# Two graph-network layers by nested fast matrix products: S4 written graph by graph, two sums of y behind VectorE's adds, first aggregations mixed with the next P1, variances of the last tiles on ScalarE

## The chip, the cores and the metric

The kernel runs on one core of one Trainium2 chip. The metric is the device time of one execution in microseconds: the median of three runs before the change is 1888.36 us (1888.13 to 1889.2). All matrix products are fp32. TensorE multiplies into the eight banks of PSUM (called `bank` in the profile), VectorE (DVE) and ScalarE (ACT) read and write the banks, GpSimd (POOL) works on SBUF only, and SyncE (SP) issues the transfers.

## The reference

64 graphs of 256 nodes with 512 features, two layers, each with a residual and a layer norm. Cut to what matters:

```python
def _L0_gnn_ref(x, adj, W):
    deg = jnp.sum(adj, axis=-1, keepdims=True)
    agg = jnp.einsum('bij,bjf->bif', adj, x) / jnp.maximum(deg, EPS)
    cat = jnp.concatenate([x, agg], axis=2)
    return jax.nn.relu(jnp.einsum('bnf,of->bno', cat, W))

def _L1_gnn_ref(X, adj, mask, Wqk, Wv):
    q, k = jnp.split(X @ Wqk, 2, axis=-1)
    v = X @ Wv
    agg = jnp.einsum('bij,bjd->bid', adj, k * mask[:, :, None])
    w = inv_scale * mask * jnp.einsum('bid,bid->bi', q, agg)
    return jax.nn.softmax(w, axis=1)[:, :, None] * v

x = _layernorm(x + _L0_gnn_ref(x, adj, L0_gnn_W), axis=-1)
x = _layernorm(x + _L1_gnn_ref(x, adj, nodemask, L1_gnn_Wqk, L1_gnn_Wv), axis=-1)
```

## The kernel before: the parts that the change and the prediction touch

The graphs go through in 32 pairs. In iteration j, layer 0 of pair j and layer 1 of pair j-1 are interleaved product by product. A product with weights is done by a scheme of seven products, P1 to P7, where four of them (P1, P2, P3, P5) are split by the same scheme again. The scheme needs sums of the left side (S1 to S4) and of the right side (T1 to T4). S1 to S3 are made on VectorE or GpSimd, S4 on GpSimd. S4 is stored over a sum that is no longer needed: over S1 for the input of layer 0 (`xT_s`), over S2 for that of layer 1 (`x1T_s`).

```python
def block(self, s, ks):          # a sum or a block of the input, for graphs ks
    return self.s[:, ks, self.slot[s]] if isinstance(s, int) else self.a[:, ks, s[0], :, s[1]]

def fourth_sums(X):
    ks = slice(0, 2)
    gp.tensor_sub(X.block(S4, ks), X.block(A12, ks), X.block(S2, ks))
    inner_sums(X, gp, 2)         # four smaller sums of S4, for P3
```

The work is ordered by lists of small steps; `run("a b c")` takes the next step of each list named. A step issues one or more products (`mm`), then the copies and adds of its result, then `tick()`, which issues waiting steps of other chains (norms, masks, weight sums) to VectorE and ScalarE as far as a model of their load allows; `flush(name)` issues the rest of a chain at once.

The products P1, P2, P5 and P3 (`inner`) have four steps each. P1 and P5 end with VectorE's adds to two banks; then P1's banks `u` are copied by ScalarE, before P6 (the products with S2, `pairs(u, X, S2, ...)`) adds onto the same banks:

```python
def last_two():
    mm(q[1][:, :HF], X.chunk(block, 1, 1), b["T4"])
    mm(q[0][:, HF:], s(3), b["B22"])
    if p in ("P1", "P5"):
        for k in range(2):
            vec.tensor_add(q[k][:, HF:], q[k][:, HF:], fifth[0])   # bank<-bank,fifth
    done(fifth[0])
    tick()

def after_p1(fifth):
    for k in range(2):
        act.copy(own[:, k, 0], u[k])                               # own<-bank
```

An aggregation (`gather`) multiplies the adjacency (`adj`, with sums `sa`) with a right side (here y, with sums `tv`) by one level of the scheme, with steps a to g:

```python
def sums_T(val, later=None):
    ...
    vec.tensor_sub(t1, b12, b11)
    rest = [lambda args=args: vec.tensor_sub(*args) for args in ((t2, b22, t1), (t3, b22, b12), (t4, b21, t2))]
    if later is None:
        for do in rest:
            do()
    else:
        later.extend(rest)       # issued by spare(), one each in a, b and d

def onto(t, ps):                 # adds a bank to own, scaled by 1/degree
    for k in range(2):
        r = own[:, k, t, :HF]
        vec.scalar_tensor_tensor(r, ps[:, k * HF:(k + 1) * HF], rdeg[:, k, t:t + 1], r, op0=OP.mult, op1=OP.add)

def u1():                        # a
    twice(u, "A11", "B11")
    ...  onto(0, u)
    spare(); tick()
def g2():                        # b
    twice(p2, "A12", "B21")
    ...  onto(0, p2)
    spare(); tick()
def g5():                        # c
    twice(p5, "S1", "T1")
    tick()
def u2():                        # d: adds onto the bank of a
    twice(u, "S2", "T2", start=False)
    act.copy(r12, of(u))
    spare(); tick()
def u3():                        # e
    twice(u, "S3", "T3", start=False)
    act.copy(r22, of(u))
    vec.tensor_add(r22, of(p5), r22)
    tick()
# f = g3 (S4·B22 onto p5), g = u4 (A22·T4 onto u)
```

The main loop, cut (i, k, m, r are P1, P5, P2, P3 of layer 0; p, q, s are P6, P7, P4; j there is P1 of layer 1):

```python
for j in range(NP):
    ...
    if j == 0:
        run("i k i k i k i k", i=i, k=k)
        ...
    elif j == 1:
        early.append(a1)
        run("k i k i k i k", i=early[0], k=k)      # one step of P1 was done at j == 0
        fourth_sums(X)
        run("m p p m p p m", m=m, p=p)
        load_x(1)
    else:
        run("i k", i=i, k=k)
        ...
        run("i l k", i=i, k=k, l=open1)
        flush("norm")
        ...
        run("i k i k", i=i, k=k)
    if j != 1:
        fourth_sums(X)
    ...
    run("r q r m", m=m, q=q, r=r)
    if j == 1:
        flush("norm", "mask")
        sumsM[0] = adj_sums(0)
        load_rows(2)
    ...
    T_late = []
    T = sums_T(ys[j], T_late if j < 2 else None)
    g = gather(sumsA.pop(j), T, zs[j], pw[1], y[1], y[0], owns[j], rdegs[j], T_late)
    if j == 0:
        ...
        run("s s a b s d c e i g f", s=s, i=early[0], **g)
    elif j == 1:                                    # (an else in the kernel)
        turn_here(Y, owns[0], 0, pw)
        run("s", s=s)
        turn_here(Y, owns[0], 1, pw)
        ...
        run("s b a s d c", s=s, **g)
        ...
    else:
        run("s s j s a b", s=s, j=jj, k=k, **g)
        run("j", j=jj)
        ...
        run("c d j k e j", s=s, j=jj, k=k, **g)
```

The end, for layer 1 of the last pair: `b3` adds P3 and its fifth product (`fifth`) to v (here `x`); `probs` is the softmax; x1 (`own`) is the residual and the output.

```python
run("r", r=r)
flush()
for k in range(2):
    last[k][0](pw[k])                    # probabilities: total x fifth
b3(held[0])                              # per k: v += y[k]; v[HF:] += fifth
for k in range(2):
    vec.tensor_copy(probs[j][:, k], pw[k][:, :NT])
for t in (1, 0):
    for k in range(2):
        o = x1[:, k, t:t + 1]
        vec.scalar_tensor_tensor(o[:, 0], vs[j][k][:, t], probs[j][:, k, t:t + 1], o[:, 0], op0=OP.mult, op1=OP.add)
        stats, scale = layer_norm(o, ..., 1, (t, k) == (0, 1))    # bn_stats, bn_aggr; Ln, Exp; shift; scaling
        run_now(stats + scale[:1])
        norms.append((k, t, scale[1:]))
        if len(norms) == 2:
            close(*norms.pop(0))         # shift, scaling, transfer of the tile
close(*norms.pop(0))
```

Of the kernel before, what the change touches and what calls it, by code (L numbers as in the profile page):

```python
# [46 lines left out]
A11, A21, A12, A22 = ((u, v) for u in range(2) for v in range(2))  # L47
S1, S2, S3, S4 = range(4)
# [46 lines left out]
def resnorm_kernel(  # L95
# [15 lines left out]
    NT, NF, NA = N // P, F // P, A // P  # L111
    H, HF = NF // 2, F // 2
# [7 lines left out]
    small = ctx.enter_context(tc.tile_pool(name="small", bufs=4))  # L120
# [55 lines left out]
    def first(out, in_):  # L176

        return tc.keep_in_program_order(nc.sync.dma_start(out, in_))
# [10 lines left out]
    def load_rows(j):  # L189
        rows[j] = pool.tile([P, 2 * NT * F], F32, name="turn")[:, :2 * NT * N].rearrange(  # L190
            "p (k t n) -> p k t n", k=2, t=NT)
        for k in range(2):
            first(rows[j][:, k], adj[2 * j + k].rearrange("(t p) j -> p t j", p=P))
# [88 lines left out]

    def fourth_sums(X):

        ks = slice(0, 2)
        gp.tensor_sub(X.block(S4, ks), X.block(A12, ks), X.block(S2, ks))
        inner_sums(X, gp, 2)

    def run_now(steps):
        for _, work in steps:  # L290
            work()
# [13 lines left out]
    def adj_sums(j):  # L305
        a, s = adjs[j], pool.tile([P, 4, 2, P], F32, name="sa", bufs=2)
        a11, a21, a12, a22 = (a[:, :, t, h * P:(h + 1) * P] for t in range(2) for h in range(2))
        gp.tensor_add(s[:, 0], a21, a22)
        gp.tensor_sub(s[:, 1], s[:, 0], a11)
        gp.tensor_sub(s[:, 2], a11, a21)  # L310
        gp.tensor_sub(s[:, 3], a12, s[:, 1])
        return {"A11": a11, "A12": a12, "A22": a22, "S1": s[:, 0], "S2": s[:, 1], "S3": s[:, 2], "S4": s[:, 3]}
# [71 lines left out]
            return go  # L384
        return [unit(e) for e in range(H)]

    def sums_T(val, later=None):

        b11, b12, b21, b22 = (val[:, :, t, h * HF:(h + 1) * HF] for t in range(NT) for h in range(2))
        tv = pool.tile([P, 4, 2, HF], F32, name="tv")  # L390
        t1, t2, t3, t4 = (tv[:, r] for r in range(4))
        vec.tensor_sub(t1, b12, b11)
        rest = [lambda args=args: vec.tensor_sub(*args) for args in ((t2, b22, t1), (t3, b22, b12), (t4, b21, t2))]
        if later is None:
            for do in rest:
                do()
        else:
            later.extend(rest)
        return {"B11": b11, "B21": b21, "B22": b22, "T1": t1, "T2": t2, "T3": t3, "T4": t4}

    def gather(a, w, dst, u, p5, p2, own=None, rdeg=None, later=()):
# [69 lines left out]
        return dict(a=[u1], b=[g2], c=[g5], d=[u2], e=[u3], f=[g3], g=[u4])  # L471


    def norm_of(src, total):

        rstd, shift, less, var = (small.tile([P, NT], F32, name=x) for x in ("rstd", "shift", "less", "var"))

        def mean():
            vec.tensor_scalar(less, total, -1.0 / F, None, op0=OP.mult)

        def square(t):
            junk = small.tile([P, F], BF16, name="junk", bufs=1)
            act.activation(junk, src[:, t], AF.Square, bias=less[:, t:t + 1], accum_out=var[:, t:t + 1])

        def factor():
            act.activation(rstd, var, AF.Ln, bias=eps, scale=1.0 / F)
            act.activation(rstd, rstd, AF.Exp, scale=-0.5)

        def shifts():
            vec.tensor_tensor(shift, less, rstd, op=OP.mult)  # L490

        def scale(t):
            act.activation(src[:, t], src[:, t], AF.Identity, bias=shift[:, t:t + 1], scale=rstd[:, t:t + 1])
        return [(vec, mean)] + [(act, lambda t=t: square(t)) for t in range(NT)] + [(act, factor), (vec, shifts)] + [
            (act, lambda t=t: scale(t)) for t in range(NT)]

    def layer_norm(src, mv, n, by_vec):

# [255 lines left out]
    for j in range(NP):  # L754
# [17 lines left out]
        if j == 0:  # L772
            run("i k i k i k i k", i=i, k=k)
            flush("degrees")
            load_rows(1)
        elif j == 1:
            early.append(a1)
            run("k i k i k i k", i=early[0], k=k)
            fourth_sums(X)
            run("m p p m p p m", m=m, p=p)  # L780
            load_x(1)
        else:
            run("i k", i=i, k=k)
            send_scores(j - 2)
            run("i l k", i=i, k=k, l=open1)
            flush("norm")
            fetch_scores(j - 2)
            places[0](range(16))
            run("i k i k", i=i, k=k)
# [15 lines left out]
        flush("w0")  # L805
        run("r q r m", m=m, q=q, r=r)
        if j == 1:
            flush("norm", "mask")
            sumsM[0] = adj_sums(0)
            load_rows(2)  # L810
        quiet[0] = j < 2
        room[vec] = -9.0 if j > 1 else 0.6
        run("r s r", r=r, s=s)
# [3 lines left out]
            inner_sums(Y, gp, 0)  # L817
            queue(1, "sums", *outer_sums(Y, vec), (vec, lambda Y=Y: inner_sums(Y, gp, 1)))
        T_late = []
        T = sums_T(ys[j], T_late if j < 2 else None)  # L820

        if j == 0:
            degrees(1)
# [11 lines left out]
        if j == 0:  # L835
            sums_next()
            held = [c for c in chains if c[1] == "w1"]
            chains[:] = [c for c in chains if c[1] != "w1"]
            early.append(inner("P1", Xs[1], W0, pw[0], u, lambda fifth: early[1](fifth)))
            run("s s a b s d c e i g f", s=s, i=early[0], **g)  # L840
            quiet[0] = False
        else:
            u2, o2, y2 = o, pf, y
            b1, b2, b3, b4, b5, b6, b7, b8 = layer1(j - 1, ys[j][:, :, 0], o2, u2, y2)
            jj = inner("P1", Y, W1, pw[0], u2)
            k = inner("P2", Y, W1, y[0], o2, b2)
            if j == 1:
                turn_here(Y, owns[0], 0, pw)
                run("s", s=s)
                turn_here(Y, owns[0], 1, pw)  # L850
                inner_sums(Y, gp, 0)
                sums_Y = (*outer_sums(Y, vec), (vec, lambda: inner_sums(Y, gp, 1)))
                run("s b a s d c", s=s, **g)
                quiet[0] = False
                flush("w1")
                run("e j g f", j=jj, **g)
                queue(1, "sums", *sums_Y)
                run("k j k j k j", j=jj, k=k)
                b1(None)
                run("k", k=k)  # L860
            else:
                run("s s j s a b", s=s, j=jj, k=k, **g)
                room[vec] = 0.6
                run("j", j=jj)
                if j < NP - 1:
                    degrees(j + 1)
                run("c d j k e j", s=s, j=jj, k=k, **g)
                quiet[0] = True
                run("k", k=k)
                quiet[0] = False  # L870
                b1(None)
                run("g f", **g)
# [78 lines left out]
    for _, turn, exps in last:  # L951
        turn()
        exps()
    run("r", r=r)
    flush()
    probs[j] = small.tile([P, 2, NT], F32, name="probs", bufs=2)
    for k in range(2):
        last[k][0](pw[k])
    b3(held[0])
    for k in range(2):  # L960
        vec.tensor_copy(probs[j][:, k], pw[k][:, :NT])
    norms = []

    def close(k, t, scale):
        for _, work in scale:
            work()
        first(out[2 * j + k, t * P:(t + 1) * P], x1[:, k, t])
    for t in (1, 0):
        for k in range(2):
            o = x1[:, k, t:t + 1]  # L970
            vec.scalar_tensor_tensor(o[:, 0], vs[j][k][:, t], probs[j][:, k, t:t + 1], o[:, 0],
                                     op0=OP.mult, op1=OP.add)
            stats, scale = layer_norm(o, small.tile([P, 1, 2], F32, name="mv"), 1, (t, k) == (0, 1))
            run_now(stats + scale[:1])
            norms.append((k, t, scale[1:]))
            if len(norms) == 2:
                close(*norms.pop(0))
    close(*norms.pop(0))


# [24 lines left out]
```

## Time and profile before

| | before |
|---|---|
| median of 3 runs | 1888.36 us |
| span of the profiled execution | 1884.5 us |
| TensorE busy | 1861.3 us (99%) |
| VectorE busy | 1541.9 us (82%) |
| ScalarE busy | 1303.6 us (69%) |
| GpSimd busy | 896.5 us (48%) |
| mean granted TensorE clock | 0.997 |
| transfers | 181.26 MB, 96 GB/s in the mean |

The profile is a page of one execution, with views that can be asked for beside it: the waits (who waited for whom, total, times, longest), the chain of waits that ended last, the timeline (instructions of each engine in order of time: start, length, engine, line, operation, output<-input, shapes, how many were merged, and in brackets the idle time before and what ended it) and the instructions of one tile. The names are those of the program without buffer numbers: `xT_s` are the sums S of the input, `xT_i` the smaller sums for the inner scheme, `tv` the sums T of an aggregation, `sa` the sums of the adjacency, `own` the residual stream of a pair, `fifth` the fifth inner product. Almost all instructions carry the line of a helper, so groups are told apart by tiles.

### The profile page before, as it was taken

What the parts mean: (1) busy time and instruction counts of PE and PEld (TensorE: products, weight loads), DVE (VectorE), ACT (ScalarE), POOL (GpSimd) and SP (SyncE); (2) the same over time, 40 slices, a digit from 0 to 9 for tenths busy, and PEclk for the clock granted to TensorE, in tenths of its full rate; (3) what the DMA queues carried; (4) which work ended last, traced back from release to release, by engine and by line L of the source; (5) the groups of instructions that cost most, each with busy time, mean ns of one, the idle gap of its engine ahead of it and who ended that gap; (6) DMA issues with size and microseconds to landing.
All of it is one profiled execution on the core that took longest, in us unless ns stands there. A gap on an engine that the chain in (4) does not pass through costs nothing.

```text
span 1884.5 us, 24896 instructions
## 1 busy us (share of the span) xinstructions
PE 1861.3 (99%) x6996; PEld 1312.9 (70%) x6996; DVE 1541.9 (82%) x3182; ACT 1303.6 (69%) x3270; POOL 896.5 (48%) x1187
## 2 busy tenths in 40 slices
PE   9999999999999999999999999999999999999997
PEld 5667767767777677677677677676776777776764
DVE  7787888788888878887888888788878888878887
ACT  3667776677776677766777776777676777667765
POOL 4455453555454554435554435454445544355532
PEclk9999999999999999999999999999999999999998
DMA  6133334333333333343433343333434233433321
GB/s 225 56 74 81 99 90 118 85 97 92 103 96 103 100 83 97 90 118 85 104 88 101 96 114 89 84 98 95 112 85 108 84 102 95 118 85 88 98 62 51
DMA packets 380713, 181.26 MB, mean 96 GB/s; under 512 B 263712, under 2 KB 345248, under 8 KB 380576
## 3 DMA queue, kind: packets, MB, share of 16 engines
q1 hardware_dynamic: 380576, 179.67, 35.5%
q8 instruction: 57, 0.93, 0.2%
q14 instruction: 80, 0.66, 0.1%
HBM read 114.10 MB, written 34.06 MB: 79 GB/s over the span
## 4 chain that ended last, share of the span: by engine, by line
PE 92%; DVE 5%; ACT 1%; POOL 1%; issue 1%; DMA 0%; DVEq 0%; ACTq 0%
PE bank L173 92%; DVE own L90 2%; DVE tv L90 1%; DVE y L90 1%; POOL xT_s L90 1%; ACT y L90 0%; ACT own L90 0%; DMA wqk<-wqk_t 0%; PE bank L625 0%; ACT bank L90 0%; DVE st L90 0%; DVE t L90 0%; DVE x L90 0%; DVE v L90 0%; ACT junk L90 0%
## 5 line engine op out<-in xcount | busy, mean ns | idle before, releaser
L90 ACT COPY bank<-bank 128x256 f32<-128x256 f32 (+1 forms) x768 | 332.6, 436 | 241.0 <-PE bank L173 231.9
L90 DVE TENSOR_TENSOR y<-bank,y 128x512 f32<-128x512 f32 x256 | 170.6, 687 | 133.2 <-ACT y L90 132.2
L90 ACT ACTIVATE junk<-own,less 128x512 bf16<-128x512 f32 x252 | 182.5, 724 | 64.8 <-DVE less L90 63.9
L90 ACT ACTIVATE own<-own,shift,rstd 128x512 f32<-128x512 f32 x255 | 200.4, 812 | 0.0
L173 PE MATMUL bank<-tv,sa 128*128 128x256 f32 x768 | 194.7, 381 | 4.0 <-DVE tv L90 1.8
L90 POOL TENSOR_TENSOR x1T_s<-x1T,x1T_s 128x512 f32<-128x512 f32 x32 | 53.2, 1663 | 280.9 <-PE bank L173 280.9
L173 PEld LDWEIGHTS bank<-tv,sa 128*128 128x128 f32 x768 | 144.8, 190 | 56.0 <-issue 22.9
L90 ACT COPY y<-bank 128x512 f32<-128x512 f32 x192 | 108.9, 584 | 94.9 <-PE bank L173 93.5
L90 POOL TENSOR_TENSOR sa<-adj 128x256 f32<-128x256 f32 x128 | 95.6, 747 | 159.3 <-DMA adj<-adj_t 150.5
L173 PE MATMUL bank<-w,x1T_s 128*128 128x512 f32 (+1 forms) x384 | 168.4, 521 | 0.0
L90 POOL TENSOR_TENSOR x1T_i<-x1T 128x256 f32<-128x256 f32 x64 | 55.6, 868 | 228.6 <-DMA x1T<-turn 213.3
L173 PE MATMUL bank<-t,xT_s 128*128 128x512 f32 (+1 forms) x384 | 160.2, 526 | 2.4 <-POOL xT_s L90 1.5
L90 POOL TENSOR_TENSOR x1T_i<-x1T_s 128x128 f32<-128x128 f32 x128 | 76.6, 598 | 177.4 <-DVE x1T_s L90 174.9
L90 DVE TENSOR_TENSOR v<-bank,v 128x512 f32<-128x512 f32 x186 | 119.2, 683 | 48.8 <-PE bank L173 48.8
L173 PE MATMUL bank<-t,x1T_s 128*128 128x512 f32 (+1 forms) x384 | 158.2, 522 | 0.3 <-ACT y L90 0.3
L173 PE MATMUL bank<-w,xT_s 128*128 128x512 f32 (+1 forms) x384 | 153.2, 521 | 0.0
L173 PE MATMUL bank<-t_i,xT_i 128*128 128x256 f32 x512 | 152.7, 380 | 0.4 <-POOL sa L90 0.2
L173 PE MATMUL bank<-t_i,x1T_i 128*128 128x256 f32 x512 | 152.3, 379 | 0.1
L173 PEld LDWEIGHTS bank<-t_i,x1T_i 128*128 128x128 f32 x512 | 97.2, 190 | 67.0 <-issue 49.7
L90 ACT COPY own<-bank 128x512 f32<-128x512 f32 x128 | 71.8, 587 | 93.5 <-PE bank L173 49.4
L173 PEld LDWEIGHTS bank<-t_i,xT_i 128*128 128x128 f32 x512 | 94.9, 190 | 58.1 <-issue 46.3
L173 PE MATMUL bank<-t,x1T 128*128 128x512 f32 x256 | 130.5, 593 | 0.0
(156 smaller groups left out, 4610.1 us busy)
## 6 DMA issues: line engine op xcount, KB each, us to landing
x<-x SPq DMA_DIRECT2D x64, 512.0 KB, 5.7
xT<-x_t SPq DMA_DIRECT2D x62, 512.0 KB, 5.5
out<-own SPq DMA_DIRECT2D x62, 512.0 KB, 3.2
x1T<-turn SPq DMA_DIRECT2D x480, 64.0 KB, 2.3
adj<-adj_t SPq DMA_DIRECT2D x64, 256.0 KB, 3.8
turn<-adj SPq DMA_DIRECT2D x64, 256.0 KB, 3.0
row<-d SPq DMA_DIRECT2D x31, 256.0 KB, 4.7
wqk<-wqk_t SPq DMA_DIRECT2D x4, 512.0 KB, 5.3
```

What stands on the lines that cost most here:

```text
L90: return self.tc.keep_in_program_order(getattr(self.engine, name)(out, *args, **kwargs))
L173: tc.keep_in_program_order(nc.tensor.matmul(ps, a, b, start=start, stop=True, skip_group_check=True))
```

## The change

Six edits. S4 is subtracted for one graph after the other, so that the first half can start before the reads of the second graph's old sum are done. For the pairs from 2 on, T3 and T4 of y are issued behind VectorE's adds of the aggregation to `own` instead of ahead of them. In the first iteration S1·T1 (c) is issued ahead of S2·T2 (d), and one more step of the next pair's P1 stands between the aggregation's steps; in the second the aggregation starts with a instead of b, P2's first step comes ahead of P5's last, and the flush of the masks, the sums of the masked adjacency and a load come after the first turning of the norm's output. At the end P3's fifth product is added by an identity product on TensorE, P3's adds are split, and the variances of two of the last four tiles are taken by ScalarE's square with its accumulator instead of VectorE's statistics.

```diff
     def fourth_sums(X):
-        ks = slice(0, 2)
-        gp.tensor_sub(X.block(S4, ks), X.block(A12, ks), X.block(S2, ks))
+        for k in (slice(0, 1), slice(1, 2)):
+            gp.tensor_sub(X.block(S4, k), X.block(A12, k), X.block(S2, k))
         inner_sums(X, gp, 2)
...
-    def sums_T(val, later=None):
+    def sums_T(val, later=None, n=3):
...
-        if later is None:
-            for do in rest:
-                do()
-        else:
-            later.extend(rest)
+        for do in rest[:n]:
+            do()
+        if n < len(rest):
+            later.extend(rest[n:])
...
-            run("k i k i k i k", i=early[0], k=k)
+            run("k i k i k m k", i=early[0], k=k, m=m)
             fourth_sums(X)
-            run("m p p m p p m", m=m, p=p)
+            run("p p m p p m", m=m, p=p)
...
         if j == 1:
-            flush("norm", "mask")
-            sumsM[0] = adj_sums(0)
-            load_rows(2)
+            flush("norm")
...
-        T = sums_T(ys[j], T_late if j < 2 else None)
+        T = sums_T(ys[j], T_late, 0 if j < 2 else 1)
...
-            run("s s a b s d c e i g f", s=s, i=early[0], **g)
+            run("s s a b s c d i e i g f", s=s, i=early[0], **g)
...
                 turn_here(Y, owns[0], 0, pw)
+                flush("mask")
+                sumsM[0] = adj_sums(0)
+                load_rows(2)
...
-                run("s b a s d c", s=s, **g)
+                run("s a b s d c", s=s, **g)
...
     run("r", r=r)
+    for k in range(2):
+        mm(y[k][:, HF:], ident, held[0])
     flush()
...
-    b3(held[0])
+    def add_p3(k):
+        vec.tensor_add(vs[j][k][:, 0], y[k], vs[j][k][:, 0])
+    def stt(k, t, **more):
+        vec.scalar_tensor_tensor(x1[:, k, t], vs[j][k][:, t], probs[j][:, k, t:t + 1], x1[:, k, t],
+                                 op0=OP.mult, op1=OP.add, **more)
...
+    add_p3(0)
     for k in range(2):
         vec.tensor_copy(probs[j][:, k], pw[k][:, :NT])
     norms = []
-    for t in (1, 0):
-        for k in range(2):
-            ...                      # the loop shown above
+    for k in range(2):
+        total = small.tile([P, 1], F32, name="total2", bufs=2)
+        stt(k, 1, accum_out=total)
+        steps = norm_of(x1[:, k, 1:2], total, 1)     # mean; square, Ln and Exp on ScalarE; shift; scaling
+        run_now(steps[:3])
+        norms.append((k, 1, steps[3:]))
+    add_p3(1)
+    for k in range(2):
+        stt(k, 0)
+        stats, scale = layer_norm(x1[:, k, 0:1], small.tile([P, 1, 2], F32, name="mv"), 1, k == 1)
+        run_now(stats)
+        close(*norms.pop(0))
+        run_now(scale[:1])
+        norms.append((k, 0, scale[1:]))
+    for norm in norms:
+        close(*norm)
```

More of the change, by code (lines that the diff above doesn't have):

```diff
@@ L471, in gather, with norm_of @@
         return dict(a=[u1], b=[g2], c=[g5], d=[u2], e=[u3], f=[g3], g=[u4])
-    def norm_of(src, total):
-        rstd, shift, less, var = (small.tile([P, NT], F32, name=x) for x in ("rstd", "shift", "less", "var"))
+    def norm_of(src, total, n=NT):
+        rstd, shift, less, var = (small.tile([P, n], F32, name=x) for x in ("rstd", "shift", "less", "var"))
         def mean():
@@ L493, in scale @@
             act.activation(src[:, t], src[:, t], AF.Identity, bias=shift[:, t:t + 1], scale=rstd[:, t:t + 1])
-        return [(vec, mean)] + [(act, lambda t=t: square(t)) for t in range(NT)] + [(act, factor), (vec, shifts)] + [
-            (act, lambda t=t: scale(t)) for t in range(NT)]
+        return [(vec, mean)] + [(act, lambda t=t: square(t)) for t in range(n)] + [(act, factor), (vec, shifts)] + [
+            (act, lambda t=t: scale(t)) for t in range(n)]
     def layer_norm(src, mv, n, by_vec):
@@ L958, in resnorm_kernel, with close @@
         last[k][0](pw[k])
-    b3(held[0])
+    def add_p3(k):
[3 more added lines that the diff above has]
+                                 op0=OP.mult, op1=OP.add, **more)
+    def close(k, t, scale):
+        run_now(scale)
+        first(out[2 * j + k, t * P:(t + 1) * P], x1[:, k, t])
+    add_p3(0)
     for k in range(2):
@@ L962, in resnorm_kernel @@
     norms = []
[L964 to L967, printed above, removed]
-    for t in (1, 0):
-        for k in range(2):
[L970 to L978, printed above, removed]
+    for k in range(2):
[14 more added lines that the diff above has]
+        close(*norm)
 def kernel(x, adj, nodemask, L0_gnn_W, L1_gnn_Wqk, L1_gnn_Wv):
```

## The prediction

> **What bounds the kernel now.** I read the page first. TensorE is busy in 99% of the span, the others in 82% or less, so only TensorE's idle time, and what lies after its last matmul, can be won.
>
> ```profile
> PE 1861.3 (99%) x6996; PEld 1312.9 (70%) x6996; DVE 1541.9 (82%) x3182; ACT 1303.6 (69%) x3270; POOL 896.5 (48%) x1187
> ```
>
> Then the waits of TensorE (total, times, longest):
>
> ```profile
> PE bank L173 <- DVE tv L90: 1.8, 1, 1.8
> ...
> PE bank L173 <- POOL xT_s L90: 1.5, 9, 0.2
> ...
> PE bank L173 <- DVE own L90: 1.1, 1, 1.1
> ```
>
> They are small because the ends of matmuls are modelled. Starts tell more: in undisturbed stretches each record of 256 columns starts 0.215 us after the one before, each of 512 columns 0.43 us, and a product in the program is two records. I took from each pair of successive starts in the trace what goes beyond that. It comes to 34 us: 10 in the first 100 us, 21.5 in the steady part, 3 after 1836 us. The steady part has three places in a pair of graphs:
> - before the first product of S2 (t,xT_s): 19 of 30 pairs, about 0.3 us and a late second record each, 7.2 us in all;
> - in the first steps of P5 (t,xT_i), 0.2 us in each pair, 5.9 us, behind ScalarE's copy of a bank;
> - inside the first aggregation, between T1·S1 and T2·S2 (tv,sa), in ten pairs, 3.45 us in all.
>
> The first place is what "POOL xT_s" in the waits points at. Here is a pair with the gap, from the timeline (start, length, engine):
>
> ```profile
> 1726.79 0.92 DVE L90 TENSOR_TENSOR v<-v,fifth 128x256 f32<-128x256 f32 x1
> ...
> 1728.63 1.27 POOL L90 TENSOR_TENSOR xT_s<-xT,xT_s 128x512 f32<-128x512 f32 x1 [1.20 <-PE bank L173]
> ...
> 1728.86 1.39 DVE L90 TENSOR_TENSOR bank<-bank,fifth 128x256 f32<-128x256 f32 x4
> ...
> 1729.28 1.07 ACT L90 COPY own<-bank 128x512 f32<-128x512 f32 x2 [1.57 <-DVE bank L90]
> ...
> 1730.01 1.96 PE L173 MATMUL bank<-t,xT_s 128*128 128x512 f32 x4 [0.17 <-POOL xT_s L90]
> ```
>
> and one without:
>
> ```profile
> 1671.57 1.27 POOL L90 TENSOR_TENSOR xT_s<-xT,xT_s 128x512 f32<-128x512 f32 x1 [1.85 <-PE bank L173]
> ...
> 1672.62 1.88 PE L173 MATMUL bank<-t,xT_s 128*128 128x512 f32 x4
> ```
>
> In the second the product starts at 1672.62, while GpSimd's S4 runs until 1672.84. So the product doesn't wait for S4. In every pair with the gap the first copy of own ends 0.14 us before the product, to the hundredth; S4 ends anywhere from 0.21 before to 0.06 after it. The wait is for ScalarE's copy of u, which is behind VectorE's adds to the banks, which are behind `v<-v,fifth`, 0.92 us here and 0.42 to 0.46 in the pair without the gap.
>
> The third place:
>
> ```profile
> 1516.60 1.10 DVE L90 TENSOR_TENSOR tv<-y 128x512 f32<-128x512 f32 x1
> ...
> 1518.35 0.68 DVE L90 TENSOR_TENSOR tv<-y 128x512 f32<-128x512 f32 x1
> ...
> 1518.95 0.68 DVE L90 TENSOR_TENSOR tv<-y,tv 128x512 f32<-128x512 f32 x1
> 1519.32 2.28 PE L173 MATMUL bank<-tv,sa 128*128 128x256 f32 x8
> ...
> 1519.55 1.65 DVE L90 SCALAR_TENSOR_TENSOR own<-bank,rdeg,own 128x256 f32<-128x256 f32 x4
> ```
>
> The eight matmuls take 2.28 us instead of 1.88 (seven starts and a last one of 0.38): T2·S2 adds onto the bank that the adds to own must have read. T3 (1518.35) and T4 (1518.95) stand ahead of those adds, and no product needs them yet.
>
> **What the Trainium skill says.** "Perfetto Trace Analysis", section "Tensor Engine Instruction (MATMUL, LD_WEIGHTS)": the end of a matmul in a profile is a model, not an observation. The trace agrees: records of 0.38 us start 0.215 apart, hence my use of starts. "SBUF — State Buffer", section "Who interferes with whom": a VectorE instruction with two SBUF inputs contends with a GpSimd instruction that reads SBUF, and whichever issues first holds the pair for its whole length; with one SBUF input it doesn't. The trace agrees: `v<-v,fifth` takes 0.424 us at least and 1.014 at most, `own<-z,rdeg,own` 0.47 to 1.50, while `v<-bank,v`, with one input in a bank, stays at 0.68 to 0.69. "Perfetto Trace Analysis", section "Optimizing Scalar/DVE Operations": breaking up an instruction may let work be completed sooner if an engine isn't saturated but causes bubbles. GpSimd's 128x512 takes 1.27 us and its 128x256 0.73, so two halves cost 0.19 us more. "PSUM — Partial Sum Buffer", section "The four PSUM rules": a matmul without the first flag adds to what the bank holds; that is how the identity product can add the fifth. Before's trace has no such add to compare.
>
> **The change part by part.**
>
> *S4 by graph.* 64 subtractions of 1.27 us or more become 128 of about 0.73: 64 x 0.19 = 12 us more on an engine that is idle half the time. For xT the first half waits for one product of P5 less, so S4 ends about 0.55 us earlier; for x1T the first half moves some 3.5 us ahead, beside VectorE's T sums, and the second blocks `own<-z` half as long. No matmul waits for either. I give it 0, for the gap at S2 has another cause.
>
> *Later sums.* For pairs from 2 on, T3 and T4 go behind the adds of own. VectorE reaches those adds two times 0.61 us = 1.2 earlier, or when the first aggregation's product is done; the gap is 0.3 us plus a 0.11 restart. So all ten vanish: 3.4 us. T3 is then ready about 0.7 us after the adds, two products or more before its use.
>
> *First aggregations.* At pair 0:
>
> ```profile
> 46.83 2.94 PE L173 MATMUL bank<-tv,sa 128*128 128x256 f32 x12 [1.76 <-DVE tv L90]
> ```
>
> The wait is for T2, which is slow (1.65 us, beside GpSimd). S1·T1 needs T1 alone and now goes into the wait: 0.86 of 1.93 us. But u4 then has only one product of P1 ahead of it (0.43 us) while ScalarE reads the bank, where it had 0.86: 0.4 back. So 0.45, and 0.15 at the restart after it. With two steps of P1 done ahead, and P2's first step ahead of P5's last, the 0.27 waits at 53.78 and 58.88 and some restarts go: 0.6. At pair 1:
>
> ```profile
> 80.12 0.86 DVE L90 SCALAR_TENSOR_TENSOR own<-bank,rdeg,own 128x256 f32<-128x256 f32 x2
> ...
> 81.03 2.94 PE L173 MATMUL bank<-tv,sa 128*128 128x256 f32 x12 [1.15 <-DVE own L90]
> ```
>
> T2·S2 waits for u's adds behind those of the other bank, because b runs ahead of a. With a ahead of b they start at 78.2, T2 ends at 80.2 instead, and the wait shrinks by 0.8. Moving the masks' flush should help little: in the timeline the last two masks (69.85) are ahead of the own scalings (70.66), so ticks had issued them already. I give 0.3 of the 0.83 at 71.44. Sum of the head: 0.45 + 0.15 + 0.6 + 0.8 + 0.3 = 2.3 us.
>
> *The end.*
>
> ```profile
> 1870.29 1.05 PE L648 MATMUL bank<-total,fifth 1*128 1x1 f32 x8
> ...
> 1871.31 0.43 DVE L90 TENSOR_TENSOR x<-x,fifth 128x256 f32<-128x256 f32 x1
> ...
> 1872.37 0.42 DVE L90 TENSOR_TENSOR x<-x,fifth 128x256 f32<-128x256 f32 x1
> ...
> 1872.90 0.75 DVE L90 SCALAR_TENSOR_TENSOR own<-x,probs,own 128x512 f32<-128x512 f32 x1
> ...
> 1880.27 0.55 DVE L90 TENSOR_SCALAR own<-own,rstd,shift 128x512 f32<-128x512 f32 x1
> ```
>
> Two identity products (0.86 us, from 1869.95) push the probabilities' matmuls from 1870.29 to 1870.8, done at 1871.85. VectorE has one add (0.66) by then, copies, and starts the first weighted add at 1872.1: 0.8 earlier. From there before took 7.9 us to the end of the last scaling: four tiles of 1.62 (add 0.79, statistics 0.73, aggregate 0.10), then factor, shift, scaling. After: adds 0.9 each with their mean for two tiles, the second P3 add 0.62, then two tiles of 1.62, ending at +5.8 instead of +6.6. But ScalarE now runs scale(1,1), 0.73, ahead of the last factor, 0.5, and the last scaling (0.55) follows: +7.9 again. So the end gains 0.8, all at its start, and the last transfer (3.7 us) stays.
>
> Sum: 3.4 + 2.3 + 0.8 = 6.5; 1888.4 - 6.5 = 1881.9.
>
> **The rivals.** (1) S4 does hold the S2 products, as the chain of waits has it ("POOL xT_s" 0.9% of the span). Then halving it removes 7.2 us more: 1875. For it: the ends of S4 lie near the starts in all 19 pairs. Against: the pairs without gap start before S4 ends. (2) More GpSimd instructions, moved earlier, hit VectorE's two-input adds at worse moments, and the S2 gap appears in all 30 pairs: 11 x 0.37 = 4 us back, 1886. For it: the gap comes from just such a collision. Against: the earlier half lands beside transposes, whose lengths stay at 0.66 to 0.71. (3) T3 and T4 late make a new wait at u3 or hold VectorE for the x1T sums: each pair would lose 0.2, 6 us, and the gain is gone: 1888. Against: a slack of over 2 us at u3.
>
> **Range and chances.** The T gaps are sure to 0.5, the head to 1.2, the end to 0.6, S4 to 2 either way. 1878.5 to 1885.0 holds 8 in 10. 2% is 38 us, more than all of TensorE's 34 us of gaps: within 2% 0.98, each side 0.01.
>
> **What would show it.** The trace after: T2·S2 directly behind T1·S1 in all pairs from 2 on; the wait "DVE tv" near 1.0 and "DVE own" near 0.4; the S2 gaps still in about 20 pairs, 0.14 us behind the copy of own; the first weighted add of the last pair about 2.3 us after the last product of P3, not 2.9. Wrong if the S2 gaps are gone (rival 1), are in all pairs (rival 2), or T3 shows up as a releaser (rival 3).

## The result, and the profile after

The changed kernel takes 1903.35 us (median of four runs, 1901.88 to 1907.0) against 1888.24 us for the kernel before on the same chip: a ratio of 1.0083, with a 95% interval of 1.0065 to 1.01. It is 15 us slower, where 6.5 us less had been predicted, and lies outside the range of 1878.5 to 1885.0.

The profiled execution of the changed kernel is the slowest of its four (1907.0 us, span 1905.2; 1884.5 before), so the waits read from it add up to more than the medians differ by. Its line of busy times:

```profile
PE 1874.2 (98%) x7000; PEld 1308.8 (69%) x7000; DVE 1560.8 (82%) x3180; ACT 1307.5 (69%) x3274; POOL 909.8 (48%) x1251
```

No engine has become a bound: VectorE's 19 us more and GpSimd's 13 us more are a per cent of the span or less, and TensorE is still busy in 98% of it. What has changed shows in the chain that ended last, here by line:

```profile
PE bank L173 70%; DVE own L90 8%; DVE tv L90 3%; DVE y L90 3%; ACT junk L90 2%; DVE less L90 2%; ACT own L90 1%; DVE v L90 1%; DVE z L90 1%; DVE agg L90 1%; ACT agg L90 1%; POOL xT_i L90 1%; ACT bank L90 0%; POOL xT_s L90 0%; DVE turn L90 0%
```

TensorE's products carried 92% of this chain before, and carry 70% now. Names stand in it that the page of before doesn't list among its fifteen: `less` (minus the mean, in layer 0's norm), `agg` (the copies in layer 1's aggregation), `xT_i` (GpSimd's inner sums). The waits of TensorE (total us, number of times, longest) say where the chain comes back to it:

```profile
PE bank L173 <- ACT agg L90: 6.8, 25, 0.4
PE bank L173 <- ACT own L90: 5.6, 10, 0.8
PE bank L173 <- ACT bank L90: 2.8, 5, 1.2
```

"ACT agg" is new: 25 waits of some 0.3 us. "ACT own" is the old gap in front of the S2 products. To see all of it I again took from each pair of successive matmul starts what goes beyond the spacing of undisturbed ones (0.215 us for 256 columns, 0.43 for 512):

| us beyond back-to-back starts | before | after |
|---|---|---|
| first 100 us | 9.9 | 9.9 |
| steady part | 21.6 | 43.2 |
| - u4 of layer 1's aggregation (tv,adj), and the restarts behind it | 0 | 19.5, 25 pairs |
| - first S2 product (t,xT_s), and its restart | 7.3, 21 pairs | 12.9, 28 pairs |
| - T2·S2 in layer 0's aggregation (tv,sa) | 3.5, 10 pairs | 0 |
| - first steps of P5 | 5.9 | 5.9 |
| from 48.5 us ahead of the end to the last matmul | 2.9 | 2.7 |
| last matmul's start to the end of the span | 13.4 | 11.8 |

So the T gap went as predicted, and two things came: a wait at u4 that wasn't there at all, and more of the S2 gap. (At u4 the wait itself is 0.44 us on average; the next few matmuls start late too, which makes it 0.78 per pair. What the places listed leave of the steady part, some 4.9 us before and after alike, is mostly rounding: undisturbed starts lie nearer to 0.2155 and 0.431 us apart.)

The wait at u4 in one pair, in the timeline after (start, length, engine; lines of VectorE, GpSimd, ScalarE and TensorE in order of start):

```profile
1661.88 0.84 POOL L90 TENSOR_TENSOR x1T_s<-x1T,x1T_s 128x256 f32<-128x256 f32 x1 [4.99 <-PE bank L173]
...
1671.81 1.10 DVE L90 SCALAR_TENSOR_TENSOR own<-own,x 128x512 f32<-128x512 f32 x1
...
1672.32 1.71 POOL L90 TENSOR_TENSOR xT_s<-xT 128x512 f32<-128x512 f32 x1
...
1672.95 1.11 DVE L90 TENSOR_SCALAR less<-sum 128x2 f32<-128x2 f32 x1
...
1674.09 0.72 ACT L90 ACTIVATE junk<-own,less 128x512 bf16<-128x512 f32 x1 [1.94 <-DVE less L90]
...
1675.66 0.56 ACT L90 COPY agg<-bank 128x512 f32<-128x512 f32 x1
...
1676.27 1.13 PE L173 MATMUL bank<-tv,adj 128*128 128x256 f32 x4 [0.26 <-ACT agg L90]
```

and the same place in the timeline before:

```profile
1647.68 1.67 POOL L90 TENSOR_TENSOR x1T_s<-x1T,x1T_s 128x512 f32<-128x512 f32 x1 [9.10 <-PE bank L173]
...
1654.55 0.57 DVE L90 TENSOR_SCALAR less<-sum 128x2 f32<-128x2 f32 x1
...
1655.15 0.72 ACT L90 ACTIVATE junk<-own,less 128x512 bf16<-128x512 f32 x1 [0.59 <-DVE less L90]
...
1655.74 1.26 POOL L90 TENSOR_TENSOR xT_s<-xT 128x512 f32<-128x512 f32 x1
...
1656.72 0.57 ACT L90 COPY agg<-bank 128x512 f32<-128x512 f32 x1
...
1658.20 1.03 PE L173 MATMUL bank<-tv,adj 128*128 128x256 f32 x4
```

Read the two from the bottom. u4 adds onto a bank that ScalarE must have copied to `agg`. Two squares of layer 0's norm (`junk<-own,less`) stand ahead of that copy in ScalarE's queue, and in all 30 pairs it starts as the second of them ends (0.09 us ahead of the recorded end). The squares need `less`, two numbers per partition that VectorE makes. Before, `less` starts 1.19 us ahead of `xT_s<-xT`, GpSimd's first large sum for the next pair, and takes 0.57. After, `xT_s<-xT` starts 0.63 us ahead of `less`, which takes 1.11 and ends 0.03 behind it. The order of two neighbours has been swapped; everything behind them in the chain is 1.3 us later against TensorE, and the slack of 0.9 us that u4 had is gone.

### The profile page after: what moved, and what is told of

Its sections match the earlier page's. It is cut to its first block, busy times and chain, and to the rows that moved or that the text cites. A ratio compares the mean times of both kernels' runs of the same rounds, so it can differ in the third digit from the quotient of the medians.

```text
span 1905.2 us, 25004 instructions
## 1 busy us (share of the span) xinstructions
PE 1874.2 (98%) x7000; PEld 1308.8 (69%) x7000; DVE 1560.8 (82%) x3180; ACT 1307.5 (69%) x3274; POOL 909.8 (48%) x1251
## 4 chain that ended last, share of the span: by engine, by line
PE 70%; DVE 19%; ACT 5%; issue 4%; POOL 1%; DMA 0%; DVEq 0%; SPq 0%; POOLq 0%; ACTq 0%
PE bank L173 70%; DVE own L90 8%; DVE tv L90 3%; DVE y L90 3%; ACT junk L90 2%; DVE less L90 2%; ACT own L90 1%; DVE v L90 1%; DVE z L90 1%; DVE agg L90 1%; ACT agg L90 1%; POOL xT_i L90 1%; ACT bank L90 0%; POOL xT_s L90 0%; DVE turn L90 0%
## 5 line engine op out<-in xcount | busy, mean ns | idle before, releaser
L90 POOL TENSOR_TENSOR x1T_i<-x1T_s 128x128 f32<-128x128 f32 x128 | 98.3, 768 | 189.6 <-DVE x1T_s L90 187.1
L90 POOL TENSOR_TENSOR x1T_s<-x1T,x1T_s 128x256 f32<-128x256 f32 x64 | 51.7, 808 | 239.7 <-PE bank L173 239.7
```

The costliest lines, as they stand in the source:

```text
L90: return self.tc.keep_in_program_order(getattr(self.engine, name)(out, *args, **kwargs))
```

## The experiments

The theory formed from this: **GpSimd gets ahead**. The first half of S4 for layer 1 (`x1T_s`) waits for an earlier product only, and starts 3.5 us sooner. Then S4 as a whole ends sooner, and so does each of GpSimd's later sums, the next pair's among them; they now fall onto the end of VectorE's norm, and hold `less`. The rivals: **the early half itself**, which hits another VectorE instruction where it now lies; **GpSimd's additional work** (two instructions of 128x256 cost more than one of 128x512, whenever they come); **the other parts** of the change; and, for the S2 gap, the halves of layer 0's S4 or GpSimd's sums of the adjacency (`sa`).

All medians, with the ratio to the kernel before on the same chip:

| what runs | us | before | ratio, 95% |
|---|---|---|---|
| before + S4 in halves | 1911.68 | 1887.5 | 1.0126 [1.0111, 1.0141] |
| after, S4 whole | 1883.63 | 1887.5 | 0.9983 [0.9974, 0.9992] |
| after, halves in layer 0 alone | 1885.58 | 1887.5 | 0.9989 [0.998, 0.9998] |
| after, halves in layer 1 alone | 1901.19 | 1887.5 | 1.0073 [1.0058, 1.0088] |
| after, layer 1's second half first | 1882.03 | 1887.05 | 0.9973 [0.9961, 0.9986] |
| after, next pair's S1 in halves too | 1891.94 | 1887.05 | 1.0025 [1.0016, 1.0035] |
| after, one product more between u3 and u4 | 1916.05 | 1887.05 | 1.0149 [1.0134, 1.0165] |
| S4 whole, load of adj issued earlier | 1883.6 | 1887.05 | 0.9981 [0.9974, 0.9989] |
| S4 whole, sums of adj later | 1877.24 | 1887.33 | 0.9946 [0.9934, 0.9959] |
| after, sums of adj later | 1892.93 | 1887.33 | 1.0028 [1.0017, 1.0039] |
| before + late T3 and T4 | 1883.83 | 1887.33 | 0.9983 [0.9975, 0.9991] |
| S4 whole, sums of adj later, old head | 1875.19 | 1887.33 | 0.9937 [0.9922, 0.9952] |

### Which part costs the time

S4 in halves put into the kernel before, alone:

```diff
-        ks = slice(0, 2)
-        gp.tensor_sub(X.block(S4, ks), X.block(A12, ks), X.block(S2, ks))
+        for k in (slice(0, 1), slice(1, 2)):
+            gp.tensor_sub(X.block(S4, k), X.block(A12, k), X.block(S2, k))
```

> The kernel before with S4 written graph by graph in both layers and nothing else. Theory A (the halves of S4 cost all of it, by collisions of GpSimd with VectorE's two-input and small instructions): the new wait for ScalarE's copy of agg (tv,adj, 19.5 us with its restarts in the trace after) and the longer waits ahead of the S2 products (5.6 us more) appear here too, the T2 waits of 3.4 us stay: 1888 + 25 = 1910 to 1914. Theory B (the late T3 and T4 shift VectorE and so cause the new wait): no wait for the copy of agg, 1888 to 1890.

and taken out of the kernel after (the same lines the other way round):

> The changed kernel with S4 written for both graphs in one instruction again. Theory A: the wait for the copy of agg is gone in all pairs, the S2 waits are back at about 7 us with their restarts, the T2 waits stay gone, the end keeps its 0.8 us: 1883 to 1885. Theory B: 1900 or more.

Measured: 24.2 us slower than before, and 3.9 us faster than before. The halves are the whole loss, and the other parts together gain. In the first, the wait at u4 is in 29 pairs and takes 22.0 us with its restarts; in the second one wait is left, at one pair. In the waits of TensorE, after with S4 whole:

```profile
PE bank L173 <- ACT agg L90: 0.8, 1, 0.8
```

Then layer by layer, from after:

```diff
-        for k in (slice(0, 1), slice(1, 2)):
+        halves = (slice(0, 1), slice(1, 2)) if X.name == "xT" else (slice(0, 2),)
+        for k in halves:
```

> The changed kernel with S4 in halves for layer 0's sums (xT_s) alone. Theory A: only the S2 waits grow, 1884 + 5.6 = 1889 to 1890, no wait for the copy of agg. If the two places feed each other by the time at which GpSimd's sums run, there are some waits for agg too and the time is 1892 or more.

and with `"x1T"` in the place of `"xT"`:

> The changed kernel with S4 in halves for layer 1's sums (x1T_s) alone. Theory A: the wait for the copy of agg in about 25 pairs, S2 waits as in the kernel before: 1884 + 19.5 = 1903 to 1904. If layer 0's halves cause the agg wait, 1884 to 1886.

Measured from after with S4 whole: layer 0's halves cost 1.9 us (one of its twelve runs took 4008 us; without it the median is 1885.42), layer 1's 17.6. Together that is 19.5, against 19.0 for both (15.1 slower than before, where S4 whole is 3.9 faster). The two intervals overlap, so the 1.9 alone isn't sure; the traces bear it out. Layer 1's halves bring the wait at u4 in 21 pairs, 16.2 us with restarts, and 2.1 us more at S2; layer 0's bring none of the first, and 2.7 us more at S2, about half of what was expected of them.

### Early, or more?

The same two instructions, the same total, but nothing early: the half that waits for the later product goes first, and GpSimd, which works in order, holds the other behind it (S4 then starts at 5.41 us and not at 1.96, in the table below).

```diff
-        for k in (slice(0, 1), slice(1, 2)):
+        halves = (slice(0, 1), slice(1, 2)) if X.name == "xT" else (slice(1, 2), slice(0, 1))
+        for k in halves:
```

> The changed kernel, but layer 1's S4 with the second graph's half first, so that the early half can't start before the last read of S2. Theory A1 (the early start brings all of GpSimd's later sums forward, and they hit VectorE's end of the norm chain): the sums of the next x start as late as before the change, the wait for the copy of agg is gone or in a few pairs only, 1885 to 1889. Theory A2 (more and shorter GpSimd instructions as such collide more often): the wait stays, 1900 to 1905.

Measured: 1882.03, as fast as with S4 whole, and no wait at u4 is left. It isn't the work: 64 instructions of 128x256 in layer 1 cost nothing where they end late. Its timeline at the same pair:

```profile
1645.91 2.00 POOL L90 TENSOR_TENSOR x1T_s<-x1T,x1T_s 128x256 f32<-128x256 f32 x2 [8.44 <-PE bank L173]
...
1652.24 0.57 DVE L90 TENSOR_SCALAR less<-sum 128x2 f32<-128x2 f32 x1
...
1654.12 1.26 POOL L90 TENSOR_TENSOR xT_s<-xT 128x512 f32<-128x512 f32 x1
...
1656.44 1.03 PE L173 MATMUL bank<-tv,adj 128*128 128x256 f32 x4
```

`less` is ahead of `xT_s<-xT` again, by 1.88 us. The positions in all pairs, as medians in us from the first 128x512 product of layer 1's S2 (t,x1T_s); before, all 30 pairs lie within 0.16 us of them:

| | before | after | S4 whole | second half first | S1 in halves too |
|---|---|---|---|---|---|
| S4 starts | 5.41 | 1.96 | 5.41 | 5.41 | 1.96 |
| S4 done | 7.08 | 6.13 | 7.07 | 7.40 | 6.13 |
| first sum for the next pair starts | 9.51 | 8.98 | 9.51 | 10.24 | 8.89 |
| next pair's S1 (xT_s<-xT) starts | 13.46 | 12.39 | 13.46 | 13.61 | 12.39 |
| VectorE's second `less` starts | 12.28 | 13.02 | 12.27 | 11.74 | 13.01 |
| its length | 0.57 | 1.11 | 0.57 | 0.57 | 0.57 |
| ScalarE's copy to agg starts | 14.44 | 15.72 | 14.44 | 13.91 | 15.18 |
| u4 starts | 15.93 | 16.34 | 15.93 | 15.93 | 15.93 |

Down the column "after": S4 is done 0.95 us earlier, the next pair's S1 starts 1.07 earlier, `less` ends 1.28 later (0.74 at its start, 0.54 in its length), the copy to agg is 1.28 later, u4 0.41. The 0.74 come from two VectorE instructions just ahead of `less`, which run beside GpSimd's sums for the next pair: `own<-own,x` takes 1.10 instead of 0.83 and `own<-z,rdeg,own` 1.02 instead of 0.47 (medians), while VectorE had been 0.08 ahead. The early half itself isn't the cause: it does hold one of VectorE's T sums (`tv<-own,tv`, 1.22 instead of 0.68), but VectorE's first `less` starts at 8.18, where before it was 8.27.

The pairs of the kernel after show it among themselves. In 25 of its 30 the next pair's S1 starts at 12.38 to 12.54, `less` takes 1.11 and u4 starts late, at 16.33 to 16.5. In four S1 starts at 13.24 or later, `less` is ahead of it and takes 0.56 or 0.57, and u4 starts at 15.93. In the last there is no next pair: 0.17, and 15.93 again. No pair is an exception.

### The link between S1 and `less`

If `less` is held for as long as S1 runs, a shorter S1 must release it sooner:

```diff
-            run_now(rest[:1])
+            for ks in (slice(0, 1), slice(1, 2)):
+                run_now(outer_sums(Xs[j + 1], gp, ks)[:1])
```

> The changed kernel with the next pair's S1 (128x512 on GpSimd) also written graph by graph. If it is this one long instruction that holds VectorE's small mean (less, 1.1 us instead of 0.2 to 0.6) and through it ScalarE's squares and the copy of agg: the mean waits 0.7 us at most, the copy comes about 0.5 us earlier, the wait for it goes in most pairs, 1886 to 1893. If the mean is only the last of many small delays: 1900 or more.

Measured: 1891.94, 10.2 us less than after, each against its own before. `less` starts where it did (13.01), takes 0.57 instead of 1.11, and nothing but this shift of 0.54 is passed on to the copy (15.18); it is enough for u4 (15.93). The timeline at the same pair:

```profile
1659.05 1.86 POOL L90 TENSOR_TENSOR xT_s<-xT 128x256 f32<-128x256 f32 x2
1659.68 0.57 DVE L90 TENSOR_SCALAR less<-sum 128x2 f32<-128x2 f32 x1
...
1661.85 0.56 ACT L90 COPY agg<-bank 128x512 f32<-128x512 f32 x1
...
1662.60 1.03 PE L173 MATMUL bank<-tv,adj 128*128 128x256 f32 x4
```

What remains against S4 whole is 4.8 us in 22 waits one step further on (the next P5 products of layer 1, t_i,x1T_i), and an S2 gap of 11.6 us.

The other way to give the copy time is to take u3, whose result it copies, one product (0.86 us) earlier, so that two instead of one product of P7 stand between u3 and u4:

```diff
-            run("a n b q d q n c q e q n p g f", n=n, q=q, p=p, **g)
+            run("a n b q d q n c e q q n p g f", n=n, q=q, p=p, **g)
```

> The changed kernel with u3 one product (0.86 us) earlier in the second aggregation, so that two instead of one product of P7 stand between u3 and u4, and the copy of agg is issued ahead of one of the two squares. If TensorE loses its time there only because that copy stands behind squares that wait for VectorE: no wait for agg is left, the longer waits at S2 stay, 1903 - 19 = 1884 to 1889. If the delay just moves to a later wait: 1895 or more.

This missed: 13.9 us slower than after. The wait at u4 is gone, but it has moved. The waits of TensorE:

```profile
PE bank L173 <- ACT bank L90: 28.0, 27, 1.4
```

What TensorE now waits for is a bank copy of P5 behind it in ScalarE's queue, about 1.3 us in 22 pairs of the steady part (5 of the 27 waits, 2.8 us, were there in after). ScalarE is late as a whole, and a later product pays for it. So it isn't u4's place in the order that is at fault. Why the wait costs more at P5 than at u4 was not pursued.

### The S2 gap

Left over is the gap in front of the S2 products, 6.5 us with S4 whole. The prediction laid it to `v<-v,fifth`, an add of two SBUF tiles on VectorE. In the timeline after, a pair in which it is at its largest:

```profile
523.91 0.73 POOL L90 TENSOR_TENSOR sa<-adj 128x256 f32<-128x256 f32 x1
523.95 0.97 DVE L90 TENSOR_TENSOR v<-v,fifth 128x256 f32<-128x256 f32 x1
...
525.55 0.73 POOL L90 TENSOR_TENSOR xT_s<-xT,xT_s 128x256 f32<-128x256 f32 x1
525.56 1.00 DVE L90 TENSOR_TENSOR v<-v,fifth 128x256 f32<-128x256 f32 x1
...
528.86 1.53 PE L173 MATMUL bank<-t,xT_s 128*128 128x512 f32 x3 [0.80 <-ACT own L90]
```

Each of two adds is hit: the first by a sum of the adjacency, the second by the first half of layer 0's S4, by a hundredth of a microsecond. Which of them matters without the halves? First I tried to have the sums done before the adds, with the load of adj asked for earlier (S4 whole):

```diff
+        if j > 0:
+            load_adj(j)
         flush("finish")
-        if j > 0:
-            load_adj(j)
```

> All of the change but the halves of S4, and in each iteration the load of the adjacency is queued ahead of the output's transfers, which wait for ScalarE. GpSimd's sums of the adjacency then run some 2.6 us earlier, before VectorE's v + fifth adds. If those adds' collision with the sums is what delays ScalarE's copy of u and the S2 products: both v + fifth adds take 0.42 us in all pairs, the S2 waits of 6.5 us go, 1884 - 6 = 1877 to 1879. If S4 or the transposes hold S2: 1883 to 1885.

This run doesn't decide: the transfers of the output had been issued before that point already, so the queue kept its order, the adjacency came when it had come, and the time is that of S4 whole (1883.6). Then the other way, the sums behind the adds, after S4:

```diff
-            sumsA[j] = adj_sums(j)
+            if j == 1:
+                sumsA[j] = adj_sums(j)
 ...
         if j != 1:
             fourth_sums(X)
+        if j > 1:
+            sumsA[j] = adj_sums(j)
```

> All of the change but the halves of S4, and from pair 2 on GpSimd makes the sums of the adjacency behind S4 and its inner sums, some 7 us later, when VectorE's two v + fifth adds are over; no instruction of another engine changes its place. If their collision with those sums delays ScalarE's copy of u: the adds take 0.42 us always, the S2 waits (4.9 + 1.6 us) go, 1883.6 - 6.5 = 1877. If S4 or the transposes hold the S2 products: 1883 to 1885. If the later sums hit other adds that matter: 1885 or more.

Measured: 1877.24, 6.2 us below S4 whole, and the S2 gap is gone but for 0.3 us in one pair. S4 is whole here and ends 0.29 us behind the start of the S2 product (median), so that product doesn't wait for it. The group `v<-v,fifth` of VectorE (minimum, median, maximum in ns) with S4 whole:

```profile
L90 DVE TENSOR_TENSOR v<-v,fifth x62: 424/426/923, 119.2 to 1838.1; 128x256 f32<-128x256 f32 x62
```

and with the sums of adj later:

```profile
L90 DVE TENSOR_TENSOR v<-v,fifth x62: 424/426/426, 118.2 to 1830.7; 128x256 f32<-128x256 f32 x62
```

Not one of 62 is held any more. The same move in the kernel after, with its halves:

> The whole change, with the sums of the adjacency behind S4 and its inner sums as in the run before. If the two waits have two causes: the S2 waits (10.7 + 2.2 us) go though S4 is in halves, the wait for agg (19.5 us) stays: 1903.4 - 12.9 = 1890. If the halves of layer 0's S4 hold S2 by themselves: 1898 to 1903.

Measured: 1892.93, 9.5 us less than after. The adds are free there too, and the S2 gap falls from 12.9 us to 0.3 in one pair, though layer 0's first half is still early: without the sums the first add is some 0.55 us shorter, so the second is done before the half comes. The wait at u4 stays, in 19 pairs instead of 25, 14.7 us with restarts.

The two causes are thus separate, and each can be removed alone.

### Late sums, and a kernel that is faster than both

The late T3 and T4 put into the kernel before, alone (the change's own `sums_T(val, later=None, n=3)`):

```diff
-        T = sums_T(ys[j], T_late if j < 2 else None)
+        T = sums_T(ys[j], T_late, 0 if j < 2 else 1)
```

> The kernel before with T3 and T4 of y behind the adds of own from pair 2 on, and nothing else. The T2 waits (3.45 us in ten pairs) go and no other wait comes: 3.4 us less than before, 1883.7 beside 1887.1. If VectorE's idle moment ahead of those adds costs elsewhere: 1887 or more.

Measured: 3.5 us faster, where the prediction had 3.4. Last, the sums of adj later with pairs 0 and 1 ordered as before the change (so: late T3 and T4, the new end, S4 whole, sums of adj later):

```diff
-            run("k i k i k m k", i=early[0], k=k, m=m)
+            run("k i k i k i k", i=early[0], k=k)
 ...
-            run("s s a b s c d i e i g f", s=s, i=early[0], **g)
+            run("s s a b s d c e i g f", s=s, i=early[0], **g)
 ...
-                run("s a b s d c", s=s, **g)
+                run("s b a s d c", s=s, **g)
```

> As the first run of these, but with pairs 0 and 1 ordered as in the kernel before. In the trace after, the head's waits for T2 shrink by 1.8 us and a new wait of 1.4 us for ScalarE's bank copy at 57.7 us comes: the head is worth 0.3 us or nothing, the same as that run within 0.5 us. If the new order of the head does pay: 1.5 us slower or more.

Measured: 1875.19 (1874.92 to 1875.37), 12.1 us below the kernel before and 2.05 below the same kernel with the new head. It is the fastest of all that were run, and neither of the two outcomes expected: the new head costs time. Of the 2.05, 1.3 is the one wait at u4, with its restarts, that the kernels with the new head and layer 1's S4 whole have (near 680 us, one pair: `xT_s<-xT` ahead of `less`, 1.71 and 1.11 us long as in after, and 0.96 us at u4), and 0.3 the last S2 gap. In that pair GpSimd gets ahead without any halves. From the timeline with the sums of adj later:

```profile
667.70 1.26 POOL L90 TENSOR_TENSOR x1T_s<-x1T,x1T_s 128x512 f32<-128x512 f32 x1 [8.44 <-PE bank L173]
...
667.90 1.60 DVE L90 TENSOR_TENSOR y<-y,fifth 128x512 f32<-128x512 f32 x1 [0.46 <-ACT adj L90]
```

VectorE's add starts 0.35 us later than in the other pairs, and behind S4 instead of ahead of it. S4 then takes 1.26 us instead of 1.67 and is done 0.41 sooner, at 6.67 instead of 7.08 from the pair's first S2 product. Why that add starts late was not found.

## Why the prediction was wrong

- **S4 by graph: the step that failed.** "For x1T the first half moves some 3.5 us ahead, beside VectorE's T sums", "No matmul waits for either", "I give it 0". The 3.5 us are right (5.41 to 1.96), and no matmul does wait for S4 itself. But the step followed the half only to its own end. GpSimd's queue is in order: what it had to do after S4 moved forward with it, out of the place where VectorE could bear it. The term was 0 and measured +19 us (after against after with S4 whole), +24 in the kernel before. The early half by itself left VectorE's first `less` no later; the sums behind it, 0.5 to 1.1 us sooner, held the second, and u4 waited in 25 of 30 pairs.
- **What S4 was thought to be about.** That S2 doesn't wait for S4 holds: with S4 in halves for layer 0 the gap at S2 grew (9.3 us against 6.5) instead of closing, and with S4 whole and the sums of adj moved it closed. Rival 1 is out. (Counted as here, the kernel before has the gap in 21 pairs and not 19, and S4 ends up to 0.17 us after the product in them and not 0.06; the reading stands.)
- **Rival 2** named the right kind of cause, GpSimd's instructions at worse moments, and was right on the S2 gap (28 of 30 pairs; 5.6 us more than before, where it had 4). It looked for it only where a gap already was. The greater part, 19.5 us, came at a place that had none, and the link that decides there wasn't one of the "two-input adds" but a 128x2 instruction, with two held two-input instructions ahead of it. What was said against this rival, that the earlier half lands beside transposes, doesn't hold: layer 1's lands beside `tv<-own,tv` (1.22 us), layer 0's beside `v<-v,fifth` (1.00 us in the pair shown).
- **That link contradicts what the prediction said of VectorE.** It had that an instruction with one SBUF input doesn't contend. `less<-sum` has one, and takes 0.155 to 1.11 us. The Trainium skill, "SBUF — State Buffer", section "Who interferes with whom", does say that a `tensor_scalar` (not the form that writes out its accumulator) can enter a two-port mode and contend too, and that issue order decides who blocks; the prediction left out the page's condition, "outside the 2-port perf modes". Which mode `less` ran in no trace shows, but that it contends they do: `less` ends 0.03 us behind the GpSimd instruction ahead of it, both at 0.57 and at 1.11, and takes 0.627 at most where S1 is in halves.
- **Breaking up.** The Trainium skill, "Perfetto Trace Analysis", section "Optimizing Scalar/DVE Operations", has, of ScalarE and VectorE, that breaking up may let work be completed sooner; the prediction took this over to GpSimd. The work was completed sooner, by 0.95 us, and that was the harm.
- **Late sums: right** (3.4 predicted, 3.5 measured alone, with a 95% interval of 1.7 to 4.7, and no T gap in the steady part of after). Rival 3 is out: T3 is no releaser in the waits.
- **The head: wrong in its sum** (2.3 predicted; the excess of the first 100 us is 9.9 before and after). The two waits for T went as predicted, 1.93 to 1.07 and 1.31 to 0.35, and the new 0.41 at u4 came too. But the "0.6" for two waits of 0.27 turned into a new one of 1.41. In the timeline of after with S4 whole:

```profile
57.99 0.76 DVE L90 TENSOR_TENSOR bank<-bank,fifth 128x256 f32<-128x256 f32 x2
...
58.46 1.27 ACT L90 COPY own<-bank 128x512 f32<-128x512 f32 x2 [1.69 <-DVE bank L90]
...
59.62 0.59 ACT L90 COPY bank<-bank 128x512 f32<-128x512 f32 x1
...
60.27 0.70 PE L173 MATMUL bank<-t_i,xT_s 128*128 128x256 f32 x2 [1.24 <-ACT bank L90]
```

  With P1 done early, its two copies of u stand in ScalarE's queue ahead of P5's bank copy, and wait there for VectorE's adds. The masks' 0.83 is where it was; the 0.3 given for it was wrong.
- **The end: right.** From the last step of P3 to the end of the last scaling before took 11.75 us, after takes 10.78: 1.0 against 0.8 predicted. The two identity products put the probabilities' matmuls off to 1.88 us behind the start of that step (1890.73 to 1892.61), where before it was 1.22 (1869.07 to 1870.29); yet the first weighted add comes after 3.04 us (1893.77) and not after 3.83 (1872.90). All the gain but 0.2 lies at this start, as the step had it. The two starts in the timeline after:

```profile
1892.61 1.05 PE L647 MATMUL bank<-total,fifth 1*128 1x1 f32 x8
...
1893.77 0.74 DVE L90 SCALAR_TENSOR_TENSOR own<-x,probs,own 128x512 f32<-128x512 f32 x1
```

- **The range** took the S4 term as 0 with 2 us either way, from the one gap it was thought able to touch. With that term at its measured +19 and the head at about 0, the rest of the sum (late sums 3.4, end 0.8) leads to 1903.0, beside 1903.35. The +19 is itself taken from that 1903.35; what was measured apart from it is that everything else together gives 3.9 us (S4 whole), beside 3.4 + 0.8.

## What to carry to other kernels

When an instruction of an engine that works in order is split so that its first part can start earlier, follow that engine's queue on to the next point where it waits for something else: all of it moves, and each piece has to be held against what it can collide with at the new time (here VectorE's `less`, which took 1.11 us instead of 0.57). A split that gives nobody an operand sooner is best ordered so that it ends when it did before (here: the half that waits longest goes first, 1882.03 against 1903.35). And where a short instruction of one engine stands at the head of a chain through a second engine's queue to TensorE, place the long instructions of its rival behind it: moving one set of sums behind VectorE's adds gave more (6.2 us) than any part of the change.

## What had not been expected of the hardware

- A VectorE instruction on 128x2 numbers (0.155 us when free) lasts until 0.02 to 0.03 us after the end of the GpSimd instruction ahead of it, in all 30 pairs before the change: in after 0.57 us behind a 128x256 sum, 1.11 behind a 128x512 one.
- The collisions lock the two engines in step. `xT_s<-xT` takes 1.26 us when it runs alone and 1.71 when it starts inside `own<-own,x`, which ends at 1672.91; then it holds `less` to 1674.06. In after a pair falls into one of two patterns and not between them: the second `less` takes 0.56 or 0.57 us, or 1.11, in every pair that has a next one.
- A wait named in the profile need not be the queue that is short: "ACT agg" (25 waits) became "ACT bank" (27 waits, four times the time) when one product was moved, with the same late ScalarE behind both.
